# Attention rounds of a two-layer kernel: transposing probabilities on VectorE and moving squares inside SBUF

## The chip, the cores and the metric

The kernel runs on one core of one Trainium2 chip. That core has a matrix engine (TensorE, PE in the profile), three other compute engines (VectorE or DVE, ScalarE or ACT, GpSimd or POOL), and SyncE (SP), which in this program issues all DMA transfers. Each engine takes its instructions in the order in which they were written into its stream and waits at one until its inputs are there. The metric is the device time of the whole program in microseconds: 882.81 us, the median of three runs of the kernel before (882.34 to 883.55).

## The reference

Eight sequences of 128 tokens with 512 features pass two layers, each a cross-attention on a context `ctx_4096` of the same shape and a feed-forward block, every one on a layernormed input and added to the stream:

```python
x = x + _L0_xattn_ref(_layernorm(x, axis=-1), ctx_4096, ...)
x = x + _L0_ffn_ref(_layernorm(x, axis=-1), ...)
x = x + _L1_xattn_ref(_layernorm(x, axis=-1), ctx_4096, mask, ...)
x = x + _L1_ffn_ref(_layernorm(x, axis=-1), ...)
```

What matters here is the second cross-attention. It has 32 query heads of 128 dimensions that share 8 key/value heads (four query heads to a group), with RMS norm on queries and keys, scores plus a mask, softmax, the product with the values, and an output projection from 4096 back to 512. The feed-forward block after it takes 4-bit integer weights with a zero point and a scale for each group of 128 rows: gate, up and down projections of 512 x 1792, and silu(gate) * up between them.

## The kernel before

The first layer and the key/value projections of the second take the first 220 us. Most products are computed to nearly float32 accuracy from float32r halves: a tensor is cut into a high part (a copy in float32r) and a low part (the difference), and `mm3` (L73) makes three matmuls, low x high, high x high and high x low. Such cuts are done by ScalarE and VectorE (`split_fast`) or by POOL alone (`split_pool`).

The second cross-attention runs over 64 units, a unit being one key/value group and one sequence (its 4 query heads at once). `round_(n)` (L749) issues the steps of several units in the order of the list `ROUND` (L738); each entry has an offset, the unit it works for being n plus that offset. The whole stage stands under a manual schedule, so every engine gets its instructions in the order of these calls. The steps of a unit before the change, with the offset at which they run:

- `q_mm` (offset 4): query projection, 12 matmuls of 128 x 512; `q_ssq` (4): squares summed by ScalarE; `q_rms` (3): the inverse root on POOL.
- `q_turn` (3): VectorE scales the queries and transposes them in squares of 32 x 32 (L517, L523) into `qb`. Squares lie transposed, but still on the partitions of their rows.
- `q_write` (3) and `q_read` (2): the squares go to DRAM in one transfer of 256 KB, and come back in four of 64 KB to the partitions where they belong. The read is issued one round after the write.
- `s_mm` (1): four score products (L543), a further round later; `s_max` (1) adds the mask and takes the maximum on VectorE, `s_exp` (1) is ScalarE, `s_norm` (1) divides by the sum, on POOL (L565).
- `p_mm` (1): PE transposes the probabilities, four transposes of 128 x 128 (L570), at the end of the round; `p_cut` (0) cuts them on ScalarE and VectorE (L574, L575) from PSUM.
- `av_mm` (0): three matmuls with the values; `av_cut` (0): the result is cut on ScalarE and VectorE (L591, L592), with a reordering of its columns; `o_mm` (0): the output projection, 12 matmuls; `o_add` (0): the sum into the stream (L604).

The string entries stand for loads and cuts of weights, which are spread over the rounds: `"load"` issues DMAs for the q and o weights and every fourth round for keys and values, `"cut"` cuts weights on POOL, `"int"` and `"sub"` load the integer weights of the feed-forward stage with their zero points and write their difference to DRAM (`int_dma`, `int_sub`). The last four rounds take `TAIL`, which has no `q_mm`. In rounds 53 to 57 and in the last ones the layernorm of finished sequences is woven in, and `fillers` puts the first gate and up units of the feed-forward stage (its first `NE` chunks, for the first four sequences) between the steps. All DMA issues stand in one queue, SP's, in the order of the calls.

The prelude (L791) interleaves the last two groups of keys and values with the first queries. The stage after the attention is the feed-forward block, ordered by `emit` for most chunks and written out by hand for the last ones.

Of the kernel before, what the change touches and what calls it, by code (L numbers as in the profile page):

```python
# [9 lines left out]
F32 = mybir.dt.float32  # L10
# [7 lines left out]
P = 128  # L18
# [21 lines left out]
def tile_layers(ctx: ExitStack, tc: tile.TileContext, t, out: bass.AP):  # L40
# [76 lines left out]
    NE = 3  # L117
# [342 lines left out]
    qps, qss, rqs, qbs, q_d, qTs, sps, nms, sms, prs, tps, pTs, avs, aTs, pos = ({} for _ in range(15))  # L460
# [20 lines left out]
    def k_load(g, hf):  # L481

        kTt[g, hf] = pk.tile([P, NQ, HB, SQ], F32, name="kT")
        for k in range(NQ):
            nc.sync.dma_start(
                kTt[g, hf][k * SQ : (k + 1) * SQ].rearrange("p i b a -> p i (b a)"),
                kT_d[g, hf][:, k, :].rearrange("(i c) e -> c i e", c=SQ),
            )

    def v_load(g, hf):  # L490
        for i, (d, p) in enumerate(((vht, "h"), (vlt, "l"))):
            d[g, hf] = pv.tile([P, HB, HD], F32R, name=f"v{p}")
            nc.sync.dma_start(f32(d[g, hf]).rearrange("p b d -> p (b d)"), v_d[g, hf][i])
# [33 lines left out]
    def q_write(u):  # L527
        q_d[u] = dram.tile([P, NQ, NREP * SQ], F32, name=f"q_d{u}")
        nc.sync.dma_start(q_d[u], qbs.pop(u).rearrange("p j r a -> p j (r a)"))

    def q_read(u):

        qTs[u] = wk.tile([P, NQ, NREP * SQ], F32, name="qT", bufs=8)
        for j in range(NQ):
            nc.sync.dma_start(
                qTs[u][j * SQ : (j + 1) * SQ], q_d[u][:, j, :].rearrange("(i c) e -> c i e", c=SQ)
            )
# [29 lines left out]
    def p_mm(u):  # L567
        tp = tps[u] = ps_tr.tile([P, NQ, P], F32, name="tr")
        for r in range(NQ):
            nc.tensor.transpose(tp[:, r, :], prs[u][:, r, :], ident)  # L570

    def p_cut(u):
        ph, pl = pTs[u] = tuple(pat.tile([P, NQ, P], F32R, name=f"pT_{p}") for p in "hl")
        nc.scalar.copy(ph, tps[u])  # L574
        nc.vector.tensor_tensor(pl, tps[u], f32(ph), ALU.subtract)  # L575
# [10 lines left out]
    def av_cut(u):  # L586
        ah, al = aTs[u] = tuple(pat.tile([P, NREP, P], F32R, name=f"aT_{p}") for p in "hl")

        src = avs[u].rearrange("p i (r a) -> p r i a", a=SQ)
        hp, lp = (x.rearrange("p r (i a) -> p r i a", a=SQ) for x in (ah, al))  # L590
        nc.scalar.copy(hp, src)  # L591
        nc.vector.tensor_tensor(lp, src, f32(hp), ALU.subtract)  # L592
# [18 lines left out]
    def int_dma(m, c):  # L611
        wi, zi = (
            wk.tile([P, NREP, P], F32, name="qT", bufs=8).bitcast(I32).rearrange("p r c -> p (r c)")
            for _ in range(2)
        )
        staged[m, c] = (wi, zi)
        if m == "down":
            nc.sync.dma_start(wi, t["down_w"][c * P : (c + 1) * P, :])
            nc.sync.dma_start(zi, t["down_z"][c : c + 1, :].to_broadcast([P, D]))
        else:  # L620
            cols = slice(c * P, (c + 1) * P)
            nc.sync.dma_start(
                wi.rearrange("p (g c) -> p g c", c=P), t[m + "_w"][:, cols].rearrange("(g p) c -> p g c", p=P)
            )
            nc.sync.dma_start(
                zi.rearrange("p (g c) -> p g c", c=P), t[m + "_z"][:, cols].unsqueeze(0).to_broadcast([P, KT, P])
            )
# [16 lines left out]
    def early_unit(m, g, c):  # L644
# [9 lines left out]
        if g % 2 == 0:  # L654
            et[m, c, g] = wk.tile([P, NREP, P], F32, name="qT", bufs=8).rearrange("p r c -> p (r c)")
            nc.scalar.activation(et[m, c, g], ps, AF.Copy, scale=s)
        else:
            d = et[m, c, g - 1]
            if m == "gate" and g == 1:
                a2 = wk.tile([P, NREP, P], F32, name="qT", bufs=8).rearrange("p r c -> p (r c)")  # L660
                nc.scalar.activation(a2, ps, AF.Copy, scale=s)
                nc.gpsimd.tensor_tensor(d, d, a2, ALU.add)
            else:
                nc.vector.scalar_tensor_tensor(d, ps, s, d, ALU.mult, ALU.add)
# [55 lines left out]
    def norm_turn(b):  # L720
        hf, i = divmod(b, HB)
        if i == 0:
            xn2[hf] = tuple(big.tile([P, KT, TOK], F32R, name=f"xnT_{p}") for p in "hl")
        layernorm_t(xnb[b], *xn2[hf], slice(i * P, (i + 1) * P), ps_q, tag="mm")


    FILL = {(NU - 1, p_cut): 3, (NU - 1, s_norm): 2}
    for n in range(NU - 4, NU - 1):
        FILL[n, p_cut], FILL[n, s_norm] = 1, 3 if n == NU - 2 else 2
    BANKS = "qst" "qst" "qsqt" "qstqs" "tqstqos" "to"  # L730
    xn2, xnb, xst = {}, {}, {}
    norms = {}
    for b in range(NB):
# [5 lines left out]
        (1, s_mm), (3, q_rms), (0, p_cut), (4, q_mm, (0,)), (1, s_max), (0, av_mm), "int", (2, q_read),  # L739
        (0, av_cut), (3, q_turn), (4, q_mm, (1, 2, 3)), (1, s_exp), "load", (3, q_write), "cut", "sub",  # L740
        (0, o_mm), (1, s_norm), (4, q_ssq), (1, p_mm), (0, o_add),
    ]

    TAIL = [
        (1, s_mm), (3, q_rms), (0, p_cut), (1, s_max), (0, av_mm), (2, q_read), (0, av_cut), (3, q_turn),
        (1, s_exp), (1, s_norm), "load", (3, q_write), (0, o_mm), (1, p_mm), (0, o_add),
    ]

    def round_(n):  # L749
        for it in ROUND if n < NU - 4 else TAIL:  # L750
            if isinstance(it, str):
                for fn, a in tasks.get((n, it), []):
                    fn(*a)
            elif 0 <= n + it[0] < NU and not (n == 0 and it[1] is q_read):
                it[1](n + it[0], *it[2:])
# [34 lines left out]
    with tc.manual_schedule():  # L790
        for u, (g, hf) in enumerate(((NG - 2, 0), (NG - 2, 1), (NG - 1, 0))):  # L791
            kv_part(g, hf, 0)
            if u:
                q_rms(u - 1)
                q_turn(u - 1)
                q_write(u - 1)
# [3 lines left out]
            q_ssq(u)  # L800
            if u == 0:
                kv_cut(NG - 1)
            else:
                q_read(u - 1)
                for k in ((0, 1), (2, 3))[u - 1]:
                    load_dma("o", 0, k)
        s_mm(0)
        s_max(0)
        s_exp(0)
        s_norm(0)  # L810
        kv_part(NG - 1, 1, 0)
        q_rms(2)
        q_turn(2)
        q_write(2)
        kv_part(NG - 1, 1, 2)
        q_mm(3, range(KT))
        kv_out(NG - 1, 1)
        q_read(2)
# [9 lines left out]
        for k in range(KT):  # L828
            wo[0, k] = o_first[(k + 1) % KT]
        for k in (0, 1):  # L830
# [4 lines left out]
        p_mm(0)  # L835
# [5 lines left out]
        fillers(len(fill) - 2)  # L841
# [72 lines left out]
    def gated(c):  # L914
        th = ths.pop(c)
        tp = part(th, c)
        nc.vector.tensor_tensor(tp, tp, part(gu["up", 0], c), ALU.mult)
# [3 lines left out]
        nc.scalar.copy(part(hh, c), tp)  # L921
# [37 lines left out]
    def emit(seq, i):  # L959
        c = ORDER[i] if i < NI else NI  # L960
        for it in seq.split():
# [9 lines left out]
            elif k in "SHL" and c < NI:  # L971
                {"S": silu, "H": gated, "L": rest}[k](c)

    for i in range(NI - 1):
# [3 lines left out]
        emit(f"g0 d0 g2 g1 u0 g3 gm d1 u2 {a}u1 d3 d2 u3 um S" + (" H L" if i < NI - 2 else ""), i)  # L978
    ET = mybir.EngineType
    with tc.manual_schedule(engines={ET.PE, ET.DVE, ET.Activation, ET.Pool}):  # L980
# [14 lines left out]
        rest(ORDER[-2])  # L995
        downs("A")
        up_unit("up", 0, c)
        silu(c)
        up_unit("up", 1, c)
# [4 lines left out]
        gated(c)  # L1004
        downs("AV")
# [66 lines left out]
```

## Time and profile before

| | |
|---|---|
| median of three runs | 882.81 us (882.34 to 883.55) |
| the profiled execution: its own time | 884.13 us |
| its span, first to last instruction | 882.3 us |
| PE busy | 852.1 us |
| DVE, POOL, ACT busy | 626.7, 517.5, 438.7 us |
| PE busy from 293 to 629 us (45 rounds) | 335.93 of 336.00 us |
| DMA share in that stretch | 0.74 |
| transposes of probabilities (L570), 256 of them | 40.1 us busy, 279 ns each |
| score products (L543), 512 passes | 68.0 us busy, 276 ns each |

Busy time is the time in which an engine had an instruction in flight. Matmuls overlap on PE, so that the durations of a group add up to more than the group holds PE; what a group costs is read from the distance between the starts of what stands before and after it. A row of a timeline has the start in the span, the duration, engine, line, operation and the tiles written and read; in brackets stands the idle time of the engine before it and what ended it. A DMA row shows the issue on SP (SPq); the time to landing is told from the start of the issue.

### The profile page before, as it was taken

What the parts mean: (1) busy time and instruction counts of PE and PEld (TensorE: products, weight loads), DVE (VectorE), ACT (ScalarE), POOL (GpSimd) and SP (SyncE); (2) the same over time, 40 slices, a digit from 0 to 9 for tenths busy, and PEclk for the clock granted to TensorE, in tenths of its full rate; (3) what the DMA queues carried; (4) which work ended last, traced back from release to release, by engine and by line L of the source; (5) the groups of instructions that cost most, each with busy time, mean ns of one, the idle gap of its engine ahead of it and who ended that gap; (6) DMA issues with size and microseconds to landing.
All of it is one profiled execution on the core that took longest, in us unless ns stands there. A gap on an engine that the chain in (4) does not pass through costs nothing.

```text
span 882.3 us, 14414 instructions
## 1 busy us (share of the span) xinstructions
PE 852.1 (97%) x4568; PEld 716.2 (81%) x4568; DVE 626.7 (71%) x1049; ACT 438.7 (50%) x1565; POOL 517.5 (59%) x571
## 2 busy tenths in 40 slices
PE   6999999999999999999999999999999989999976
PEld 5889999899787888888888888888778767788764
DVE  6613797775766677777777677666786887888877
ACT  5324444243544454455544444445555668666652
POOL 4551684234565455555555555775554568899884
PEclk9999999999999999999999999999999999999999
DMA  8522441435787788878788886644344412222103
GB/s 295 138 96 97 143 145 72 134 105 168 237 253 227 221 245 240 218 242 243 229 237 239 243 238 210 187 145 138 110 129 144 132 34 73 72 72 72 48 13 109
DMA packets 141182, 141.07 MB, mean 160 GB/s; under 512 B 17969, under 2 KB 92465, under 8 KB 141105
## 3 DMA queue, kind: packets, MB, share of 16 engines
q1 hardware_dynamic: 141104, 140.14, 53.3%
q8 instruction: 37, 0.61, 0.3%
q14 instruction: 41, 0.33, 0.1%
HBM read 97.62 MB, written 42.47 MB: 159 GB/s over the span
## 4 chain that ended last, share of the span: by engine, by line
PE 79%; DVE 6%; POOL 5%; DMA 5%; issue 2%; ACT 2%; SPq 1%; DVEq 0%; ACTq 0%; POOLq 0%
PE mm L74 8%; PE mm L76 8%; PE mm L75 8%; PE f L870 6%; PE f L871 6%; PE o L76 6%; PE s L543 6%; PE o L75 6%; PE o L74 6%; PE tr L570 3%; PE kv L76 3%; PE kv L75 3%; PE kv L74 3%; DMA qT<-q_d 2%; PE o L584 1%
## 5 line engine op out<-in xcount | busy, mean ns | idle before, releaser
L565 POOL TENSOR_TENSOR pr<-pr,rs 128x512 f32<-128x512 f32 x64 | 66.6, 1040 | 179.6 <-DVE rs L563 176.7
L604 DVE TENSOR_TENSOR xs<-o,xs 128x512 f32<-128x512 f32 x64 | 44.2, 691 | 95.5 <-PE o L76 95.5
L74 PE MATMUL mm<-wq_l,xnT_h 128*128 128x512 f32 x256 | 105.4, 412 | 0.0
L76 PE MATMUL o<-wo_h,aT_l 128*128 128x512 f32 x256 | 100.0, 391 | 0.7 <-DVE aT_l L592 0.7
L74 PE MATMUL o<-wo_l,aT_h 128*128 128x512 f32 x256 | 100.1, 391 | 0.2 <-DVE wo_l L66 0.2
L76 PE MATMUL mm<-wq_h,xnT_l 128*128 128x512 f32 x256 | 100.2, 391 | 0.0
L75 PE MATMUL mm<-wq_h,xnT_h 128*128 128x512 f32 x256 | 100.0, 391 | 0.0
L75 PE MATMUL o<-wo_h,aT_h 128*128 128x512 f32 x256 | 99.7, 390 | 0.0
L574 ACT CAST pT_h<-tr 128x512 fp32r<-128x512 f32 x64 | 37.5, 585 | 121.2 <-PE tr L570 121.2
L557 ACT ACTIVATE pr<-s,nm 128x128 f32<-128x128 f32 x256 | 90.8, 373 | 3.2 <-DVE nm L551 3.0
L591 ACT CAST aT_h<-o 128x512 fp32r<-128x512 f32 x64 | 37.6, 587 | 106.9 <-PE o L584 106.9
L74 PE MATMUL kv<-wkv_l,cT_h 128*128 128x256 f32 x256 | 73.6, 288 | 0.0
L508 ACT ACTIVATE junkq<-mm 128x128 f32<-128x128 f32 x256 | 67.3, 279 | 12.4 <-PE mm L76 6.1
L76 PE MATMUL kv<-wkv_h,cT_l 128*128 128x256 f32 x256 | 73.3, 286 | 0.0
L75 PE MATMUL kv<-wkv_h,cT_h 128*128 128x256 f32 x256 | 72.9, 285 | 0.0
L543 PE MATMUL s<-kT,qT 128*128 128x128 f32 x512 | 68.0, 276 | 1.9 <-DMA qT<-q_d 1.9
L348 POOL TENSOR_TENSOR rrq<-msq,nhalf 128x4 f32<-128x4 f32 x64 | 64.7, 1011 | 5.3
L543 PEld LDWEIGHTS s<-kT,qT 128*128 128x128 f32 x512 | 62.3, 192 | 3.0 <-DMA qT<-q_d 2.8
L575 DVE TENSOR_TENSOR pT_l<-tr,pT_h 128x512 fp32r<-128x512 f32 x64 | 44.0, 688 | 22.8 <-ACT pT_h L574 22.8
L76 PEld LDWEIGHTS o<-wo_h,aT_l 128*128 128x128 f32 x256 | 48.1, 188 | 11.6 <-DVE aT_l L592 1.5
L76 PEld LDWEIGHTS mm<-wq_h,xnT_l 128*128 128x128 f32 x256 | 48.1, 188 | 10.7
L74 PEld LDWEIGHTS o<-wo_l,aT_h 128*128 128x128 f32 x256 | 48.1, 188 | 10.7 <-DVE wo_l L66 0.6
(234 smaller groups left out, 2445.0 us busy)
## 6 DMA issues: line engine op xcount, KB each, us to landing
q_d<-qb SPq DMA_DIRECT2D x64, 256.0 KB, 2.4
qT<-q_d SPq DMA_DIRECT2D x256, 64.0 KB, 3.1
wst<-in_qpT SPq DMA_DIRECT2D x36, 256.0 KB, 3.5
wst<-in_opT SPq DMA_DIRECT2D x36, 256.0 KB, 3.1
wkv<-in_kvT SPq DMA_DIRECT2D x8, 512.0 KB, 4.3
v_d<-vh SPq DMA_DIRECT2D x16, 256.0 KB, 2.1
v_d<-vl SPq DMA_DIRECT2D x16, 256.0 KB, 2.3
kT_d<-kT SPq DMA_DIRECT2D x16, 256.0 KB, 2.6
```

The source lines that it names most:

```text
L74: nc.tensor.matmul(o, ah, bl, start=start, stop=False)
L75: nc.tensor.matmul(o, ah, bh, start=False, stop=False)
L76: nc.tensor.matmul(o, al, bh, start=False, stop=stop)
L348: nc.gpsimd.tensor_tensor(r[:, :n], ms[:, :n], nhalf[:, :n], ALU.pow)
L508: nc.scalar.activation(junk, qps[u][:, r * HD : (r + 1) * HD], AF.Square, accum_out=ssq[:, r : r + 1])
L543: nc.tensor.matmul(sp[:, r, :], qTs[u][:, r, :], kTt[blocks[j]][:, :, i, :], start=True, stop=True)
L557: nc.scalar.activation(pr[:, r, :], sps[u][:, r, :], AF.Exp, bias=nms[u][:, r : r + 1], accum_out=sm[:, r : r + 1])
L565: nc.gpsimd.tensor_tensor(pr, pr, rs.unsqueeze(2).to_broadcast([P, NQ, P]), ALU.mult)
L575: nc.vector.tensor_tensor(pl, tps[u], f32(ph), ALU.subtract)
L604: nc.vector.tensor_tensor(x, pos[u], x, ALU.add)
L870: nc.tensor.matmul(ps[:, hf, :], w, rl, start=True, stop=False)
L871: nc.tensor.matmul(ps[:, hf, :], w, rh, start=False, stop=True)
```

## The change

- `q_write` and `q_read` become one step `q_move`: four transfers inside SBUF, each from 32 partitions of `qb` to all 128 partitions of one query head's slice of `qT`. It stands at offset 3, in the round of `q_turn`.
- The same way replaces the transposes on PE: `p_turn` lets VectorE transpose the probabilities in squares of 32 x 32, `p_move` makes the four transfers, and `p_cut` takes its input from SBUF, with POOL in place of VectorE for the low part.
- Scores, maximum, exponential and normalization stand at offset 2 in place of 1, so there is a round between normalization and `p_turn`.
- Squares now lie in another order on the partitions; keys and values are loaded in the same order (one transfer for the keys in place of four), and `av_cut` needs no reordering.
- Gate and up integer weights and zero points are laid out by the host so that a chunk is contiguous.
- `NE` is 4 in place of 3: one more chunk of the feed-forward stage has its first half computed early. `FILL` and `BANKS`, which place these fillers, are written anew, the prelude and `TAIL` follow the new offsets, and `cast` is a step of its own in the feed-forward stage.

```diff
-    NE = 3
+    NE = 4
...
     def k_load(g, hf):
-        for k in range(NQ):
-            nc.sync.dma_start(
-                kTt[g, hf][k * SQ : (k + 1) * SQ].rearrange("p i b a -> p i (b a)"),
-                kT_d[g, hf][:, k, :].rearrange("(i c) e -> c i e", c=SQ),
-            )
+        nc.sync.dma_start(
+            kTt[g, hf].rearrange("p i b a -> p i (b a)"), kT_d[g, hf].rearrange("(i c) j e -> (c j) i e", c=SQ)
+        )
...
-    def q_write(u):
-        q_d[u] = dram.tile([P, NQ, NREP * SQ], F32, name=f"q_d{u}")
-        nc.sync.dma_start(q_d[u], qbs.pop(u).rearrange("p j r a -> p j (r a)"))
-
-    def q_read(u):
-        qTs[u] = wk.tile([P, NQ, NREP * SQ], F32, name="qT", bufs=8)
-        for j in range(NQ):
-            nc.sync.dma_start(
-                qTs[u][j * SQ : (j + 1) * SQ], q_d[u][:, j, :].rearrange("(i c) e -> c i e", c=SQ)
-            )
+    def move(dst, src):
+        for i in range(NQ):
+            nc.sync.dma_start(dst[:, i, :], src[i * SQ : (i + 1) * SQ].rearrange("p j i a -> p j (i a)"))
+
+    def q_move(u):
+        qTs[u] = wk.tile([P, NQ, NREP * SQ], F32, name="qT", bufs=6)
+        move(qTs[u], qbs.pop(u))
...
-    def p_mm(u):
-        tp = tps[u] = ps_tr.tile([P, NQ, P], F32, name="tr")
-        for r in range(NQ):
-            nc.tensor.transpose(tp[:, r, :], prs[u][:, r, :], ident)
+    def p_turn(u):
+        pb = pbs[u] = wk.tile([P, NQ, NQ, SQ], F32, name="pb", bufs=1)
+        nc.vector.transpose(
+            pb.rearrange("p j i a -> p i j a"), prs.pop(u).rearrange("p i (j c) -> p i j c", c=SQ)
+        )
+
+    def p_move(u):
+        tps[u] = wk.tile([P, NREP, P], F32, name="pT")
+        move(tps[u], pbs.pop(u))
 
     def p_cut(u):
-        ph, pl = pTs[u] = tuple(pat.tile([P, NQ, P], F32R, name=f"pT_{p}") for p in "hl")
+        ph, pl = pTs[u] = tuple(pat.tile([P, NREP, P], F32R, name=f"pT_{p}") for p in "hl")
         nc.scalar.copy(ph, tps[u])
-        nc.vector.tensor_tensor(pl, tps[u], f32(ph), ALU.subtract)
+        nc.gpsimd.tensor_tensor(pl, tps[u], f32(ph), ALU.subtract)
...
     def av_cut(u):
-        src = avs[u].rearrange("p i (r a) -> p r i a", a=SQ)
-        hp, lp = (x.rearrange("p r (i a) -> p r i a", a=SQ) for x in (ah, al))
-        nc.scalar.copy(hp, src)
-        nc.vector.tensor_tensor(lp, src, f32(hp), ALU.subtract)
+        nc.scalar.copy(ah, avs[u])
+        nc.vector.tensor_tensor(al, avs[u], f32(ah), ALU.subtract)
...
     def int_dma(m, c):
...
+        nc.sync.dma_start(wi, t[m + "_w"][c * P : (c + 1) * P, :])
+        nc.sync.dma_start(zi, t[m + "_z"][c : c + 1, :].to_broadcast([P, D]))
...
-    FILL = {(NU - 1, p_cut): 3, (NU - 1, s_norm): 2}
-    for n in range(NU - 4, NU - 1):
-        FILL[n, p_cut], FILL[n, s_norm] = 1, 3 if n == NU - 2 else 2
+    FILL = {}
+    for n, m in ((NU - 4, 1), (NU - 3, 1), (NU - 2, 2), (NU - 1, 2)):
+        FILL[n, s_max], FILL[n, p_cut] = m, 3
...
     ROUND = [
-        (1, s_mm), (3, q_rms), (0, p_cut), (4, q_mm, (0,)), (1, s_max), (0, av_mm), "int", (2, q_read),
-        (0, av_cut), (3, q_turn), (4, q_mm, (1, 2, 3)), (1, s_exp), "load", (3, q_write), "cut", "sub",
-        (0, o_mm), (1, s_norm), (4, q_ssq), (1, p_mm), (0, o_add),
+        (1, p_turn), (1, p_move), (2, s_mm), (3, q_rms), (4, q_mm, (0, 1)), (2, s_max), (0, av_mm), "int",
+        (0, av_cut), (4, q_mm, (2, 3)), (3, q_turn), (2, s_exp), (3, q_move), "load", "cut", (4, q_ssq),
+        (2, s_norm), "sub", (1, p_cut), (0, o_mm), (0, o_add),
     ]
     TAIL = [
-        (1, s_mm), (3, q_rms), (0, p_cut), (1, s_max), (0, av_mm), (2, q_read), (0, av_cut), (3, q_turn),
-        (1, s_exp), (1, s_norm), "load", (3, q_write), (0, o_mm), (1, p_mm), (0, o_add),
+        (1, p_turn), (1, p_move), (2, s_mm), (3, q_rms), (2, s_max), (0, av_mm), (0, av_cut), (3, q_turn),
+        (2, s_exp), (2, s_norm), (3, q_move), (1, p_cut), "load", (0, o_mm), (0, o_add),
     ]
...
     with tc.manual_schedule():
-        for u, (g, hf) in enumerate(((NG - 2, 0), (NG - 2, 1), (NG - 1, 0))):
+        for u, (g, hf) in enumerate(((NG - 2, 0), (NG - 2, 1), (NG - 1, 0), (NG - 1, 1))):
             kv_part(g, hf, 0)
             if u:
                 q_rms(u - 1)
                 q_turn(u - 1)
-                q_write(u - 1)
+                q_move(u - 1)
+            if u > 1:
+                s_mm(u - 2)
+                s_max(u - 2)
+                s_exp(u - 2)
+                s_norm(u - 2)
...
     def gated(c):
-        th = ths.pop(c)
-        tp = part(th, c)
-        nc.vector.tensor_tensor(tp, tp, part(gu["up", 0], c), ALU.mult)
+        th = hts[c] = ths.pop(c)
+        nc.vector.tensor_tensor(part(th, c), part(th, c), part(gu["up", 0], c), ALU.mult)
+
+    def cast(c):
+        th = hts[c]
         hh, hl = (fh.tile([P, 2, TOK], F32R, name=f"h_{p}") for p in "hl")
```

## The prediction

> **What bounds the kernel now.** First the page: busy times, then the chain that ended last.
>
> ```profile
> PE 852.1 (97%) x4568; PEld 716.2 (81%) x4568; DVE 626.7 (71%) x1049; ACT 438.7 (50%) x1565; POOL 517.5 (59%) x571
> ...
> PE 79%; DVE 6%; POOL 5%; DMA 5%; issue 2%; ACT 2%; SPq 1%; DVEq 0%; ACTq 0%; POOLq 0%
> ```
>
> PE fills the span and carries the chain. A busy PE need not be at its peak, so next one attention round, from the timelines of PE, ScalarE, VectorE and the DMA issues.
>
> ```profile
> 449.72 0.64 PE L570 MATMUL tr<-ident,pr 128*128 128x128 f32 x4
> 450.20 1.06 PE L543 MATMUL s<-kT,qT 128*128 128x128 f32 x8
> 451.01 0.48 PE L74 MATMUL mm<-wq_l,xnT_h 128*128 128x512 f32 x1
> 451.32 0.40 PE L75 MATMUL mm<-wq_h,xnT_h 128*128 128x512 f32 x1
> ...
> 452.25 0.40 PE L584 MATMUL o<-pT_l,vh 128*128 128x512 f32 x1
> ...
> 457.26 0.64 PE L570 MATMUL tr<-ident,pr 128*128 128x128 f32 x4
> 457.73 1.06 PE L543 MATMUL s<-kT,qT 128*128 128x128 f32 x8
> ```
> ```profile
> 452.68 0.59 ACT L591 CAST aT_h<-o 128x512 fp32r<-128x512 f32 x1 [1.70 <-PE o L584]
> ```
> ```profile
> 453.30 0.69 DVE L592 TENSOR_TENSOR aT_l<-o,aT_h 128x512 fp32r<-128x512 f32 x1 [0.26 <-ACT aT_h L591]
> 453.91 0.68 DVE L517 TENSOR_TENSOR q<-mm,rrq 128x512 f32<-128x512 f32 x1
> 454.63 0.71 DVE L523 STREAM_TRANSPOSE qb<-q 128x512 f32<-128x512 f32 x1
> ```
> ```profile
> 449.95 1.79 SPq L535 DMA_DIRECT2D qT<-q_d  x4
> ...
> 455.37 0.34 SPq L529 DMA_DIRECT2D q_d<-qb  x1
> ```
>
> A round is 457.73 - 450.20 = 7.53 us with no PE gap; transposes take 450.20 - 449.72 = 0.48 of it. The other rows show how late in a round the query squares are ready: qb ends at 455.34, 5.1 us after the scores started. They go to DRAM at 455.37, are read from 457.48, and first used by a score product at 465.26: nearly 10 us, a whole round of slack. Last, the views of the two transfers of that detour (the writes' summary, then that of both), and the chain in a stretch where a read did come late.
>
> ```profile
> DMA to landing us min/median/max: 2.0/2.4/5.1
> ```
> ```profile
> DMA to landing us min/median/max: 1.8/3.1/6.6
> ```
> ```profile
> 256.35 3.55 DMA qT<-q_d
> 259.90 0.09 issue
> 259.99 1.14 PE s L543 x8
> ```
>
> No transfer lands under 1.8 us after its issue starts, and PE stands until it does: the score starts 0.09 us after the landing.
>
> **The change, part by part.** *Removed from PE:* four transposes per unit. 64 x 0.48 = 30.7 us, all of it on the bounding engine: the PE part of a round becomes 7.53 - 0.48 = 7.05.
>
> *The query path loses its slack.* In the order of instructions built for the changed kernel, VectorE has aT_l(n), q(n+3), qb(n+3) in a row; SP then issues four moves of 64 KB; and the score products of unit n+3 are the first PE work of round n+1, right behind the 12 output products of round n. So a ring closes within one round: scores, aV of n, aT_h, aT_l, q, qb, four moves, next scores. Before, the read was issued a round later and the score another round later. Each of the four score products waits for one move, and the last decides. Its time, from one start of the fourth product to the next:
> - fourth product to the next matmul: a quarter of the 0.89 us that a score group holds PE (chain), 0.22;
> - two groups of query products come before aV now: first matmul 0.31 (451.32 - 451.01), seven at 0.227, to the start of the last aV product: 1.90;
> - to aT_h 0.43 (452.68 - 452.25), to aT_l 0.62, to q 0.61, to qb 0.72, qb itself 0.71, to SP's issue 0.03: 3.12;
> - SP from the first to the fourth issue: 1.79 less the last one's 0.43, or 1.44 in the next round; 1.40;
> - the landing, L; and 0.09 to the product.
>
> Sum 6.73 + L. L is not shown, since no transfer inside SBUF is in this trace. Nearest rows: a read of 64 KB from DRAM, 1.8 us at best, 3.1 in the median (it stands behind the integer loads of its round); a write of 256 KB to DRAM, 2.0 at best. Without DRAM at either end it may be quicker: I bound L below by 1.3 (half a microsecond off the best row, an estimate) and above by 3.1. I take 1.85, near the quiet 64 KB row, because in the new order the integer loads go out some 3 us before the moves and little is queued ahead. Then a round is 8.58 us, of which PE waits 1.53.
>
> Sum: before, the score products of rounds 0 and 61 start at 220.72 and 686.09 (timeline), 465.4 us for 61 rounds (7.63 with the slower ones, where layernorm transposes join). After: 61 x 8.58 = 523.4, +58.0. The layernorm rounds stay at 8.58: 7.05 plus some 0.6 of transposes is less.
>
> [...]
>
> *VectorE:* loses pT_l (688 ns), gains the turning of the probabilities (qb's 713): nothing. p_turn waits for POOL's pr, and s_max, aT_l and q stand behind it; pr ends about 6.6 after S (the fourth product's start), p_turn runs at 7.5: covered by 0.9.
>
> *POOL:* gains pT_l from SBUF, 1292 ns as for wo_l<-wst. A round is 1.04 + 0.19 + 1.01 + 0.62 + 1.29 + 1.29 = 5.44 of 8.58; the four rounds with two weight cuts 7.35. pT_l ends near S + 7.9, its aV product starts at S + 8.58 + 2.12: 2.8 covered. Free; if the rounds were 7.05, those four would bind.
>
> *SP:* eight moves of 0.475 instead of four reads and a write, 1.6 us more in 8.58; a key load is one issue instead of four (-1.4, every fourth round). The probability moves issue at about S + 8.2, land by 11.5, and ScalarE wants them at S + 14. The integer loads behind them are subtracted a round later. Contiguous integer and key loads shorten the queue, off the path: nothing.
>
> *Ends:* the prelude computes one more score group (+0.9) and no transposes (-0.5). The last rounds save 2 x 0.48. Eight more early gate/up units move two matmuls each (0.45) from the later feed-forward stage into the tail, some into its 2.5 us of PE idle (1.19 and 1.29 near 713): -1 to -2. The reordered casts at the end: -1 to +1, taken as 0. Together -1.6.
>
> Total: +56. The profiled execution took 884.13 (span 882.3), 0.15% above the median 882.81; from the median, 939.
>
> **Clock.** Granted clock is 1.00 from 293 to 629 us with PE full, and 0.94 after 840, where PE works 29.87 of 42.30. [...]
>
> **Rivals.**
> - *The moves come late* (behind loads): L 2.6 to 3.1, rounds of 9.3 to 9.8, 985 to 1015. For: the reads' median of 3.1 under a DMA share of 0.74. Against: the new order issues them apart from the loads.
> - *Quick moves:* L 0.9 to 1.3, 61 x 0.55 to 0.95 below, 880 to 905. No row is that short.
> - *Faster:* the transposes' time is simply saved, PE 7.05 a round, 882 - 31 = 852. It needs 6.73 + L under 7.05, L under 0.32; break-even with 7.63 is L = 0.90. Against: the shortest landing shown is 1.8. For: only that SBUF to SBUF isn't shown.
> - *Probabilities late* (POOL as the bound): 7.35 in four rounds, 1 us in all, and only where the ring doesn't bind.
>
> **How the numbers follow.** Ring with L 1.3 to 2.6: 0.72; late moves 0.17; quick moves 0.06, its lower end about no change; faster 0.04; no change 0.01. Forecast 939. Range 905 (L 1.3) to 990 (L 2.7), leaving out the quick, the faster and half of the late ones. A change under 0.2% can't be told from none here: faster 0.04, same 0.01, slower 0.95.
>
> **What the new profile would show.** PE idle before the score products, released by the DMA qT<-qb, some 1.5 us a round and 90 in all; PE busy near 87%; score groups 8.6 apart; the four moves 1.8 to 2.1 from issue to landing; no L570 transposes; POOL's pT_l without anyone waiting long for it. It is wrong if moves land in under a microsecond, or if another chain (pr to p_turn to q) stretches the ring beyond what I counted.

## The result, and the profile after

The changed kernel takes 1054.48 us (1053.29 to 1057.07, 4 runs) against 882.58 (881.94 to 883.55, 4 runs) of the kernel before: 1.195 times as long, 95% interval 1.192 to 1.198. The forecast was 939, range 905 to 990. The sign was right and the size too small: +172 instead of +56. The profiled execution's span is 1051.5 us, against 882.3.

First the page of the kernel after: busy times, the clock granted to TensorE in 40 slices, the chain of work that ended last (by engine), the score products' group, and the moves (KB each, us from issue to landing).

```profile
PE 927.7 (88%) x4312; PEld 738.1 (70%) x4312; DVE 631.0 (60%) x1054; ACT 429.6 (41%) x1572; POOL 611.2 (58%) x639
...
PEclk9999999998999987998999899989899999999998
...
PE 36%; DMA 16%; DVE 14%; issue 11%; SPq 10%; POOL 8%; ACT 4%; DVEq 0%; POOLq 0%; ACTq 0%
...
L542 PE MATMUL s<-kT,qT 128*128 128x128 f32 x512 | 125.9, 341 | 89.3 <-DMA qT<-qb 74.8
...
qT<-qb SPq DMA_DIRECT2D x256, 64.0 KB, 2.1
pT<-pb SPq DMA_DIRECT2D x256, 64.0 KB, 2.9
```

PE's share of the chain fell from 79% to 36%. What came in is the ring that the prediction names: the moves (DMA), VectorE, SP's issuing. PE stands idle 89.3 us before the score products, 74.8 of them until a move of queries lands. One thing is not of the ring: PE does 256 instructions less, 31 us of work, and yet is busy 75.6 us longer (927.7 against 852.1). The page's groups say where. The score products alone are busy 57.9 us longer (125.9 against 68.0), because they now start one by one: 0.49 us for the two passes of one product (508.70 below), where all eight passes took 1.06 before. The query products are busy 39.5 us longer (345.1 against 305.6, their three groups together). These got slower, and the slices of the clock show when.

Next the timeline of one round of the kernel after, all engines (start, duration; in brackets the idle time before it and what ended that), from one group of score products to the next:

```profile
508.70 0.49 PE L542 MATMUL s<-kT,qT 128*128 128x128 f32 x2 [0.18 <-DMA qT<-qb]
...
510.88 0.40 PE L589 MATMUL o<-pT_l,vh 128*128 128x512 f32 x1
...
511.31 0.59 ACT L593 CAST aT_h<-o 128x512 fp32r<-128x512 f32 x1 [5.89 <-PE o L589]
...
511.93 0.69 DVE L594 TENSOR_TENSOR aT_l<-o,aT_h 128x512 fp32r<-128x512 f32 x1 [1.28 <-ACT aT_h L593]
...
512.54 0.68 DVE L518 TENSOR_TENSOR q<-mm,rrq 128x512 f32<-128x512 f32 x1
...
513.25 0.71 DVE L524 STREAM_TRANSPOSE qb<-q 128x512 f32<-128x512 f32 x1
...
514.03 2.49 SPq L531 DMA_DIRECT2D qT<-qb  x4
...
516.16 0.49 PE L542 MATMUL s<-kT,qT 128*128 128x128 f32 x2 [0.81 <-DMA qT<-qb]
516.83 1.10 PE L542 MATMUL s<-kT,qT 128*128 128x128 f32 x4 [0.17 <-DMA qT<-qb]
518.13 0.79 PE L542 MATMUL s<-kT,qT 128*128 128x128 f32 x2 [0.20 <-DMA qT<-qb]
```

This is the ring, term by term: 2.18 to the last value product, 0.43 and 0.62 to aT_h and aT_l, 0.61 to q, 0.71 to qb, 0.78 to the first issue. The fourth issue starts 1.89 later (514.03 + 2.49 - 0.60 for the last one), and its landing releases the fourth score product 2.21 after that. Sum 9.43 us, from 508.70 to 518.13. Each of the four score products waits for one move: they start as far apart as SP issues the moves, 0.61 to 0.69.

And the clock. The view of windows of the kernel after, on a grid of 3.413 us on which all 32 of its half-clock stretches begin (busy us of PE and matmuls, granted clock, DMA share, GB/s):

```profile
473.72:477.13 3.41, 2.06 (x10) 1.00 0.37 79
477.13:480.55 3.42, 3.32 (x10) 0.50 0.93 262
...
483.96:487.37 3.41, 2.35 (x12) 1.00 0.57 165
...
494.20:497.61 3.41, 2.25 (x10) 1.00 0.43 86
497.61:501.02 3.41, 3.27 (x9) 0.50 0.74 220
...
504.44:507.85 3.41, 2.39 (x11) 1.00 0.29 63
...
514.68:518.09 3.41, 2.14 (x9) 1.00 0.43 102
518.09:521.50 3.41, 3.37 (x9) 0.50 0.96 283
```

In the windows at full clock shown here PE stands 1.02 to 1.35 us idle, in one to four holes, waiting for the moves. Where it was busy 2.06 to 2.25 us of 3.41, the next window ran at half clock; after 2.35 and 2.39 it did not. A round that begins at half clock takes 10.95 us, the next 9.4, then again: 19 such windows between 300 and 700 us, mostly 20.48 apart. From the score products of round 0 (221.46) to those of round 61 (850.27) the kernel now takes 628.8 us; before it was 465.4. That is 163 of the 169 us by which the spans differ.

### The profile page after: what moved, and what is told of

The parts are those of the page before. It is cut to its first block, busy times and chain, and to the rows that moved or that the text cites. A ratio compares the mean times of both kernels' runs of the same rounds, so it can differ in the third digit from the quotient of the medians.

```text
span 1051.5 us, 14424 instructions
## 1 busy us (share of the span) xinstructions
PE 927.7 (88%) x4312; PEld 738.1 (70%) x4312; DVE 631.0 (60%) x1054; ACT 429.6 (41%) x1572; POOL 611.2 (58%) x639
## 4 chain that ended last, share of the span: by engine, by line
PE 36%; DMA 16%; DVE 14%; issue 11%; SPq 10%; POOL 8%; ACT 4%; DVEq 0%; POOLq 0%; ACTq 0%
DMA qT<-qb 12%; SPq L531 10%; PE f L858 5%; PE f L859 5%; PE mm L74 4%; PE mm L75 4%; PE mm L76 4%; PE s L542 4%; DVE q L518 4%; DVE qb L524 4%; ACT aT_h L593 3%; DMA vl<-v_d 2%; DMA pT<-pb 1%; PE o L587 1%; PE o L589 1%
## 5 line engine op out<-in xcount | busy, mean ns | idle before, releaser
L564 POOL TENSOR_TENSOR pr<-pr,rs 128x512 f32<-128x512 f32 x64 | 81.6, 1274 | 249.8 <-DVE rs L562 249.8
L542 PE MATMUL s<-kT,qT 128*128 128x128 f32 x512 | 125.9, 341 | 89.3 <-DMA qT<-qb 74.8
L542 PEld LDWEIGHTS s<-kT,qT 128*128 128x128 f32 x512 | 80.9, 203 | 146.0 <-DMA qT<-qb 132.3
L74 PE MATMUL mm<-wq_l,xnT_h 128*128 128x512 f32 x256 | 119.7, 467 | 0.0
L548 DVE TENSOR_TENSOR s<-s,mask_sb 128x512 f32<-128x512 f32 x64 | 44.6, 697 | 124.4 <-PE s L542 124.4
L75 PE MATMUL mm<-wq_h,xnT_h 128*128 128x512 f32 x256 | 112.8, 441 | 0.0
L76 PE MATMUL mm<-wq_h,xnT_l 128*128 128x512 f32 x256 | 112.6, 440 | 0.0
L594 DVE TENSOR_TENSOR aT_l<-o,aT_h 128x512 fp32r<-128x512 f32 x64 | 44.2, 691 | 111.3 <-ACT aT_h L593 111.1
L580 POOL TENSOR_TENSOR pT_l<-pT,pT_h 128x512 fp32r<-128x512 f32 x64 | 81.0, 1266 | 7.6 <-ACT pT_h L579 7.6
L74 PEld LDWEIGHTS mm<-wq_l,xnT_h 128*128 128x128 f32 x256 | 56.2, 220 | 9.8
```

Source lines behind the costliest of these rows:

```text
L74: nc.tensor.matmul(o, ah, bl, start=start, stop=False)
L75: nc.tensor.matmul(o, ah, bh, start=False, stop=False)
L76: nc.tensor.matmul(o, al, bh, start=False, stop=stop)
L542: nc.tensor.matmul(sp[:, r, :], qTs[u][:, r, :], kTt[blocks[j]][:, :, i, :], start=True, stop=True)
L564: nc.gpsimd.tensor_tensor(pr, pr, rs.unsqueeze(2).to_broadcast([P, NQ, P]), ALU.mult)
L580: nc.gpsimd.tensor_tensor(pl, tps[u], f32(ph), ALU.subtract)
```

## The experiments

In brackets stands the ratio to the kernel before, run beside each version, with its 95% interval.

**Is it the ring through the queries?** Scores that read the queries of the unit before:

```diff
-                sp[:, r, :], qTs[u][:, r, :], kTt[...]
+                sp[:, r, :], qTs[max(u - 1, 0)][:, r, :], kTt[...]
```

> The changed kernel, but each score product reads the queries of the unit before (their moves landed a round earlier); all instructions and transfers stay, the scores are of the wrong unit. Ring theory: the moves of a round no longer release its next scores, PE idle before the score products (now 75 us, released by the moves) nearly vanishes, and rounds fall from 10.3 to the next limit, PE's 7.05 or SP's issues (8 moves at 0.645 plus four others, 7.3 to 7.8): 865 to 925 us. Rival (the probabilities' way over POOL and DMA sets the round): rounds stay at 9.4 or more, over 1000 us.

Measured: 930.78 us (one run), 124 less, and a little above the range expected. Most rounds take 7.03 to 7.06 us (32 of 61 are under 7.2). Up to round 45 every fourth takes 9.5 to 13.5, the one behind the loads of keys and values. Three rounds of PE's timeline, the second of them such a long one, whose value products wait for the split of the probabilities:

```profile
497.45 1.05 PE L542 MATMUL s<-kT,qT 128*128 128x128 f32 x8
504.48 1.05 PE L542 MATMUL s<-kT,qT 128*128 128x128 f32 x8
...
508.86 0.50 PE L587 MATMUL o<-pT_h,vl 128*128 128x512 f32 x1 [1.94 <-ACT pT_h L579]
...
514.65 1.05 PE L542 MATMUL s<-kT,qT 128*128 128x128 f32 x8
...
521.68 1.05 PE L542 MATMUL s<-kT,qT 128*128 128x128 f32 x8
```

The view of waits (us in all, times, the longest):

```profile
ACT pT_h L579 <- DMA pT<-pb: 95.3, 40, 6.5
POOL pT_l L580 <- ACT pT_h L579: 71.5, 36, 5.9
```

So at least 124 of the 172 us come from the query path. Behind it stands a second limit that the prediction had as covered: the moves of the probabilities.

**What is the clock worth?** Seven matmuls that nothing reads fill PE's waits in each round: one before each score product but the first, four after the output products.

```diff
+            if r and 2 < u < NU - 12:
+                idle_mm(1)
...
+        if u < NU - 14:
+            idle_mm(4)
```

> The changed kernel with seven extra matmuls a round that nobody reads, four behind the output projection and one between score products, in PE's waits (1.6 us of work a round, up to round 49). Clock theory: the granted clock, half speed for 3.4 us out of 20.5 in the attention, stays at 1.0; the rounds of 10.9 us become 9.4 to 9.6; 1054 goes down to 995 to 1020, though PE does more. Rival (the dips are where PE waits anyway and cost nothing): unchanged, or longer by up to 50 x 1.6 = 80 us.

Measured: 1036.92 us (1.175, 1.171 to 1.180). More work for PE, and 17.6 us less time. The windows from 300 to 700 us, kernel after and then this one (busy us of PE, PEld, DVE, ACT, POOL, then the clock):

```profile
300.00:700.00 400.00, 343.72 (x1359) 261.62 (x1359) 206.29 (x348) 138.60 (x702) 224.75 (x236) 0.91 0.62 171
```
```profile
300.00:700.00 400.00, 377.42 (x1697) 290.74 (x1696) 214.57 (x362) 146.18 (x738) 236.37 (x247) 1.00 0.63 176
```

The clock is 1.00 throughout, and the term to the last value product falls from 2.92 to 2.14 (means of rounds 10 to 49). But the round only falls from 10.27 to 9.85: the issues of the four moves spread 0.12 more, they land 0.12 later, and the product waits 0.14 longer. Of these 40 rounds 24 take 9.41 in the mean, and 16 still 10.50, at full clock. That a quicker ring meets the other transfers at another point of its round is a guess; it was not tested. The clock went up as expected (1.00 for 0.91), but of the 34 to 59 us expected 17.6 came.

**What are SP's four issues in a row worth?** Two of the four query moves are issued by ScalarE:

```diff
-        move(qTs[u], qbs.pop(u))
+        move(qTs[u], qbs.pop(u), (nc.sync, nc.scalar))
```

> The changed kernel with two of the four query moves issued by ScalarE, so that the last of the four goes out after about 0.65 us and not 1.93. Ring theory: 1.25 us less in each of 61 rounds, some 975 us; down to 930 if the shorter wait also keeps the clock. Rival (DMA engines, not issues, set when the last move lands): within 1% of 1054.

Measured: 990.5 us (1.1225, 1.118 to 1.127), 64 less, where 975 was expected. The spread of the four issues falls from 1.93 to 0.72 a round, the landing rises from 2.17 to 2.84, the ring from 10.27 to 9.18. Issues of this kernel:

```profile
qT<-qb SPq DMA_DIRECT2D x128, 64.0 KB, 2.2
qT<-qb ACTq DMA_DIRECT2D x128, 64.0 KB, 2.6
```

Half of what is won in issuing is lost in landing; why the landing got longer was not followed. The clock dips less often (0.97 from 300 to 700 us), which shows in the term to the last value product: 2.41 for 2.92.

**Are moves inside SBUF dear as such?** The kernel before with its query path alone changed: the four moves in place of the write and the read, scores still one unit ahead, probabilities still transposed by PE. (The keys come in one transfer here too, as the order of the squares demands.)

```diff
-        (2, q_read), ... (3, q_write)
+        (3, q_move)
```

> The kernel before with the query path alone changed: moves inside SBUF in the round of q_turn in place of the detour over DRAM, scores still one unit ahead, probabilities still transposed by PE. The moves then have a round of slack. Ring theory: 875 to 888, as before (883) but for a few us of early waits on the reads. Rival (moves inside SBUF are dear in themselves, by issue time of 0.6 us or contention): 895 or more.

Measured: 881.39 us (879.82 to 882.65, 10 runs), ratio 0.999, 0.9975 to 1.0004: no change. Its chain, and its moves:

```profile
PE 83%; DVE 6%; POOL 5%; ACT 2%; issue 2%; DMA 1%; SPq 0%; DVEq 0%; ACTq 0%; POOLq 0%
```
```profile
qT<-qb SPq DMA_DIRECT2D x256, 64.0 KB, 2.2
```

The same moves, with the same landing, cost nothing where a round of slack lies between them and the score products.

**The slack given back to the changed kernel.** Query products, factor, turning and move one round earlier:

```diff
-        (1, p_turn), (1, p_move), (2, s_mm), (3, q_rms), (4, q_mm, (0, 1)), ... (3, q_turn), ... (3, q_move), ...
+        (1, p_turn), (1, p_move), (2, s_mm), (4, q_rms), (5, q_mm, (0, 1)), ... (4, q_turn), ... (4, q_move), ...
```

> The changed kernel with the query path one round earlier (projection five units ahead, turn and moves four), so that the moves have a round of slack again; the same work, one projection more in the prelude. Ring theory: no PE wait on the query moves; the next limit is SP's queue, 8 moves at 0.645 us, two integer loads, a weight load and a write, 7.3 a round and 9.2 in every fourth (keys, values), 7.8 in the mean against PE's 7.05: 870 to 915 us, PE waiting on late probability moves in the rounds behind key and value loads. If the moves alone were not what held the rounds: 950 or more.

Measured: 932.87 us (1.059, 1.054 to 1.063): 122 us back, with nothing left out, but above the range expected. It looks like the first experiment: 7.03 to 7.06 in many rounds, some near 8, and 9.5 to 13.3 in most of those behind the loads of keys and values:

```profile
ACT pT_h L579 <- DMA pT<-pb: 102.2, 43, 5.3
POOL pT_l L580 <- ACT pT_h L579: 73.0, 37, 4.8
```

**Another order instead of another round.** In the changed kernel, q_turn and q_move go ahead of s_max, so that the query path no longer waits for the value products of its round:

```diff
-        (1, p_turn), (1, p_move), (2, s_mm), (3, q_rms), (4, q_mm, (0, 1)), (2, s_max), (0, av_mm), "int",
-        (0, av_cut), (4, q_mm, (2, 3)), (3, q_turn), (2, s_exp), (3, q_move), "load", "cut", (4, q_ssq),
+        (1, p_turn), (1, p_move), (2, s_mm), (3, q_rms), (3, q_turn), (3, q_move), (4, q_mm, (0, 1)), (2, s_max),
+        (0, av_mm), "int", (0, av_cut), (4, q_mm, (2, 3)), (2, s_exp), "load", "cut", (4, q_ssq),
```

> The changed kernel with one step moved: VectorE turns the queries ahead of the maximum, at the start of the round, and SP issues the moves there; everything stays in its round. The ring then runs over POOL's two-round path (maximum, exponential, normalization, low part, inverse root, turn, moves), 15.2 us for two rounds, 7.6 each, with SP's 7.8 beside it: 880 to 925. If it stays over 1000, the place of the turn in the round was not the cause.

Measured: 990.29 us (one run), a miss. The moves are off the path, and a ring of VectorE and POOL is on it. Its waits from 300 to 700 us:

```profile
POOL pr L564 <- DVE rs L562: 111.8, 46, 2.6
ACT pr L556 <- DVE nm L550: 85.5, 45, 2.2
PEld o L76 <- DVE aT_l L594: 76.0, 45, 2.0
DVE q L518 <- POOL rrq L348: 67.8, 45, 2.6
```

VectorE now stands waiting for POOL's factor with the maxima and aT_l queued behind it, so PE's output products wait for aT_l: about 8.7 us in most rounds.

**The second limit.** The other runs keep the query path a round earlier and try to bring all rounds to 7.05. First, the integer and weight loads from ScalarE's queue at the end of the round:

```diff
-        nc.sync.dma_start(wi, t[m + "_w"][c * P : (c + 1) * P, :])
+        nc.scalar.dma_start(wi, t[m + "_w"][c * P : (c + 1) * P, :])
...
```

> As e5, with the integer and weight loads of the rounds issued by ScalarE at its idle end of the round; SP keeps moves, key and value loads and the write, 6.05 us a round. If SP's queue is the limit of e5, rounds fall to PE's 7.05: 61 x (7.63 - 7.05) = 35 us under the kernel before, 843 to 862, faster than both kernels. If POOL (6 us and gaps), ScalarE's added issues or the DMA engines bind first: 865 or more.

Measured: 932.42 us (1.056, 1.052 to 1.061), no gain over 932.87. The transfers' records say what the second queue left as it was. In the trace of the kernel after, each of the 925 transfers signals its landing on one of eight semaphores, and the program takes the eight in turn, so that all 917 behind the first eight have the one of the transfer eight before. The program of this version deals them out in the same way, to SP's and ScalarE's transfers alike. 900 of those 917 issues carry a wait for that earlier landing. In this trace none of the 917 goes out sooner, 28 go out within 0.2 us of it, and never more than eight transfers are under way; in the 905.70 us version below it is again none that goes out sooner, and 103 within 0.2 us. So a load ahead of a move can hold the move's semaphore until it lands. This limit is the program's. What the chip would take beyond eight no run shows, and a version with more semaphores was not tried.

The keys, high and low parts of the values in three rounds instead of one:

```diff
...
-        at(max(HB * j - 5, 1), "load", v_load, g, hf)
+        at(max(HB * j - 4, 1), "load", v_load, g, hf, (0,))
+        at(max(HB * j - 3, 1), "load", v_load, g, hf, (1,))
```

> The query path a round earlier as in the kernel with four rounds of lead, and the five or so transfers of a key and value block spread over three rounds: keys in the first, value high parts in the next, value low parts in the one after. Theory A (every fourth round of 9.5 to 13 us is made by the three big loads of one round, 0.75 MB together, which stand in front of the probabilities' moves): the excess of about 4.5 us in 15 rounds shrinks to a third or less, so 870 to 890 us. Theory B (the rounds are long because a transfer may only be issued once the one eight before it has landed, so that any load in front of the moves delays them, wherever it is put): the excess is spread over three rounds instead of one and the sum stays, 915 to 935 us.

Measured: 922.86 us (1.045, 1.042 to 1.048). Theory B: most long rounds of 9.5 to 13 went, and the others rose to about 8. Then the order as well: write-backs a round later, the big loads between the probabilities' moves and the queries', and the two integer loads issued by ScalarE:

```diff
+        (1, p_turn), (1, p_move), "out", "load", (2, s_mm), (4, q_rms), (5, q_mm, (0, 1)), (2, s_max), (0, av_mm),
+        (0, av_cut), (5, q_mm, (2, 3)), (4, q_turn), (2, s_exp), (4, q_move), "cut", (5, q_ssq),
+        (2, s_norm), "sub", (1, p_cut), "int", (0, o_mm), (0, o_add),
...
```

> As the run before, with the order of the transfers changed too: the write-back of the integer weights is issued a round after its subtraction, right behind the probabilities' moves, the weight, key and value loads follow it, so that the four query moves end the round, and the two integer loads are issued by ScalarE late in the round. Theory A (moves are late only because of what is issued in front of them in the same stretch): all rounds come to PE's own 7.05 us, 61 rounds take 430 us against 465 before, and the time is 845 to 865 us. Theory B (eight transfers before each one must have landed, whichever queue): 8 moves and 4 to 7 other transfers a round leave a move about half a round to land, rounds of 7.1 to 9 us, 880 to 925 us. Theory C (POOL, with its product at 1.3 us in place of 1.04, is next to PE): about 7.5 us a round, 870 to 885 us.

Measured: 905.70 us (1.025, 1.0195 to 1.030; its four times spread from 899.03 to 908.06), within theory B's range and the best version of the changed kernel that leaves nothing out. Many rounds are 7.03 to 7.06 now, those beside loads 7.5 to 11. SP's issues in one of the latter:

```profile
402.85 0.45 SPq L471 DMA_DIRECT2D wst<-in_qpT  x1
403.34 0.52 SPq L493 DMA_DIRECT2D vl<-v_d  x1
403.97 2.52 SPq L532 DMA_DIRECT2D qT<-qb  x4
407.12 4.37 SPq L532 DMA_DIRECT2D pT<-pb  x4
```

The first move of probabilities goes out at 407.12, the second at 409.37. The weight load issued at 402.85 landed at 407.05 and the value load of 403.34 at 409.35: they held the semaphores of the first and the second move.

Four attempts at the rest failed. The split of the moved probabilities at the start of the round that uses it:

```diff
-        (1, p_turn), (1, p_move), "out", ... "sub", (1, p_cut), "int", ...
+        (1, p_turn), (1, p_move), (0, p_cut), "out", ... "sub", "int", ...
```

> As the kernel with the new order of transfers, and one step moved: the split of the moved probabilities (its two instructions on ScalarE and POOL) opens the round whose value products use it, in place of ending the round before, so that the four moves of probabilities have about 3 us more to land. Theory A (the 61 rounds from the first one of the loop took 475.6 us there, 45 over PE's 7.05 each, because the moves land up to 5 us after their issue while loads are in flight, and a little slack absorbs that): the rounds fall to 435 to 450 us and the time to 865 to 882 us. Theory B (the transfers as a whole are too many for the round: each is issued only when the one eight before has landed, and slack only moves the wait): within 8 us of the run before, 898 to 912 us.

Measured: 915.91 us (1.039, 1.036 to 1.042), slower than both theories. The integer units spread over 56 rounds, on top:

```diff
-        at(i + 1, "int", int_dma, m, c)
+        at(1 + i * 4 // 3, "int", int_dma, m, c)
...
```

> As the run before, with the integer weights' 42 units (two loads and a write-back each, 768 KB in all) spread over 56 rounds in place of 42. Theory A (slack settles it): within 5 us of the run before. Theory B (the number of transfers in a round settles it): one unit less in every fourth round takes three of 12 to 15 transfers out of it; the long rounds get shorter in a quarter of the cases, 5 to 15 us less than the run before.

Measured: 923.32 us (1.046, 1.043 to 1.049), slower again, against both theories: more rounds at 7.05, and a few of 12 to 15. Why it is slower was not followed up. Two buffers for the squares of the probabilities (on top of the late split):

```diff
-    ppr = pool(l1s, "ppr", 2)
+    ppr = pool(l1s, "ppr", 1)
...
-        pb = pbs[u] = wk.tile([P, NQ, NQ, SQ], F32, name="pb", bufs=1)
+        pb = pbs[u] = wk.tile([P, NQ, NQ, SQ], F32, name="pb", bufs=2)
```

> As the kernel in which the split of the moved probabilities opens the round, with two buffers for the probabilities' squares in place of one (the exponentials' tile gives up its second for it). Theory A (there the transposition of the next squares by VectorE waits until the four moves have read the only buffer, so a late move holds VectorE, and with it the maxima and the queries, and the slack given to the moves is taken back): rounds of 10 to 13 us beside loads go to 8 to 9, and the time to 875 to 895 us. Theory B (ScalarE is held instead, since its two integer loads can only be issued when the transfer eight before has landed and the write-back of an older tile too): the time stays within 8 us of 916.

Measured: 916.07 us (1.037, 1.032 to 1.043): nothing. The exponentials gave up their second buffer for it, so the run shows that the trade brings nothing, not what a second buffer alone would do. And the integer loads back on SP, at the end of the round:

```diff
-        nc.scalar.dma_start(wi, t[m + "_w"][c * P : (c + 1) * P, :])
+        nc.sync.dma_start(wi, t[m + "_w"][c * P : (c + 1) * P, :])
...
```

> As the run before, with the two integer loads issued by SP at the end of the round, behind the query moves, in place of ScalarE. Theory A: SP's queue gets longer again, so the moves of the next round are issued later; within 8 us of the run before or up to 10 us slower. Theory B (ScalarE's own waits to issue are what is left): 15 to 35 us less than the run before, 865 to 890 us, and below the kernel before if it falls under 881.

Measured: 924.57 us (1.047, 1.045 to 1.049), 8.5 more: taking the loads off ScalarE brought nothing, with SP's queue longer by them.

Last, bytes against number, both from the 905.70 version. Fewer bytes in as many transfers, and as many bytes in one transfer more:

```diff
-        nc.scalar.dma_start(zi, t[m + "_z"][c : c + 1, :].to_broadcast([P, D]))
+        nc.scalar.dma_start(zi[:, 0:P], t[m + "_z"][c : c + 1, 0:P].to_broadcast([P, P]))
...
```

> The kernel with the new order of transfers (905.7 us), but of each unit's zero points only the first 128 of 512 columns are loaded, and used for all four groups of columns (so the integer weights and all that follows from them are another result): the number of transfers is the same, and 192 KB of about 1.5 MB a round are gone from the rounds that load integer weights. Theory A (the bytes of a round set its length beside loads: the attention moves about 200 GB/s here as in the kernel before, which is near what the mix allows): 192 KB at 200 GB/s are 0.96 us in 42 rounds, so up to 35 us less, 870 to 890 us. Theory B (the number of transfers sets it, since each is issued only when the one eight before has landed): landings hardly change, 895 to 910 us.

```diff
-        nc.scalar.dma_start(zi, t[m + "_z"][c : c + 1, :].to_broadcast([P, D]))
+        for h in (slice(0, D // 2), slice(D // 2, D)):
+            nc.scalar.dma_start(zi[:, h], t[m + "_z"][c : c + 1, h].to_broadcast([P, D // 2]))
```

> The kernel with the new order of transfers, with the zero points of each unit loaded by two transfers of 128 KB in place of one of 256 KB: the same bytes, one transfer more in 42 rounds. Theory A (bytes): within 6 us of 905.7. Theory B (number of transfers): one of 13 more in a round, some 0.5 us in 42 rounds, 918 to 930 us.

Measured: 892.91 us (1.012, 1.010 to 1.014) with fewer bytes, 920.50 (1.045, 1.041 to 1.049) with one transfer more: 12.8 less and 14.8 more, 0.30 and 0.35 us in each of the 42 rounds. Theory B has the second right; the first lies between the two. The 200 GB/s of theory A was no ceiling: windows shown above reach 262 and 283. Waits for the probabilities' moves from 250 to 700 us in the 905.70 version, with fewer bytes, and with one transfer more:

```profile
ACT pT_h L580 <- DMA pT<-pb: 76.0, 41, 5.7
```
```profile
ACT pT_h L580 <- DMA pT<-pb: 57.0, 35, 5.2
```
```profile
ACT pT_h L580 <- DMA pT<-pb: 100.5, 45, 4.6
```

Both move the same wait. This fits eight transfers under way at most: one transfer more takes one of the eight places, and more bytes may hold one longer. The second half of this is the author's reading, which no run shows by itself. No version of the changed kernel beat the kernel before.

Not all that is left lies in the rounds. In the 905.70 version's trace the 61 rounds take 475.6 us against 465.4; the span is 19.3 longer, and of that 3.3 lie ahead of round 0 and 5.8 behind round 61. With fewer bytes the rounds take 463.0, less than before the change, and the version is still slower, by 3.8 ahead of them and 6.8 behind.

## Why the prediction was right in sign and wrong in size

*Removed from PE*: right. With the ring opened, the rounds that wait for nothing else take 7.03 to 7.06; the step had 7.05.

*The query path loses its slack*: right as a mechanism. With the ring opened 122 to 124 of the 172 us go, and with slack the moves are free (0.999). Its sum, 8.58, was mis-sized. Means over 61 rounds, in us, from the trace of the kernel after; the predicted values are in brackets:

| Term | Measured | Predicted | Excess |
|---|---|---|---|
| fourth score product to last value product | 2.83 | (2.12) | 0.71 |
| to aT_l | 1.06 | (1.05) | 0.01 |
| q and qb, to qb's end | 2.08 | (2.04) | 0.04 |
| to the first issue | 0.07 | (0.03) | 0.04 |
| SP, first to fourth issue | 1.92 | (1.40) | 0.52 |
| landing of the fourth | 2.18 | (1.85) | 0.33 |
| to the product | 0.15 | (0.09) | 0.06 |
| round | 10.30 | (8.58) | 1.72 |

61 x 1.72 = 105 us; with the 58 foreseen, the 163 measured. Three terms failed.

- *SP from the first to the fourth issue.* The price was taken from reads out of DRAM, 1.79 for four. Four moves inside SBUF take 2.49: 0.60 each, not 0.43.
- *The landing, L.* 2.18 against 1.85 taken. The reason given for 1.85 was that little is queued ahead of the moves. That held: the median is 2.1, and none of the 256 lands under 2.07, so the excess is not a queue's. The row it was taken from, a read out of DRAM, was of another kind of transfer.
- *Clock*, in the first term. The sum allows nothing for it. But the clock halved after windows of 3.41 us in which PE was busy 2.06 to 2.25. Spread evenly over time, the 0.94 that the prediction read after 840 us would have been 0.13 a round on its 2.12 us up to the last value product (an estimate). In the windows shown the half clock falls on the stretch right behind the wait, the query products, which lie on the ring. In rounds 10 to 49 that term is 2.92, and 2.14 with the waits filled: 0.78 a round, six times as much. (Of these 40 rounds 20 have 3.67 there in the mean and 20 have 2.18.)

A fourth, smaller miss: rounds 0 and 1 take 12.06 and 14.84 us, some 6 more than two others, in places that *Ends* did not look at. In round 0 POOL splits two output weights (3.9 us) before the factor of the next queries. Round 1 ends with a wait for keys. The scores moved a round ahead, but the second block's keys are still issued in round 1, at 244.40; they land at 248.68, and unit 4's scores start at 248.82, 4.0 us after the last of their moves landed (244.79). Outside the 61 rounds *Ends* had -1.6 (with the small end of its own -1 to -2), and the trace has +6: 0.7 ahead of round 0 (221.46 against 220.72), and the rest behind round 61. From there to the first product of the feed-forward stage the kernel now takes 36.1 us, before 29.9; the stage itself is 1.3 shorter. What holds the last rounds was not followed.

*VectorE* and *POOL*: free while the ring binds, as said. POOL's pr was costed at 1040 ns as before; it takes 1274 in the mean (1379 from 300 to 700 us). The step counted four rounds with two weight cuts; rounds 2 and 3 have two as well. Neither cost anything while the ring bound.

*SP*: the moves of the probabilities were costed at nothing, covered because they land 2.5 us before ScalarE wants them. That held in the changed kernel, where ScalarE waits for them 13.4 us in all. Without the cover of a long round they are the next limit, 95 to 102 us of waiting. The step said when they land, and not what they cost once the ring is gone.

*Rivals*: the time lies nearest to "the moves come late", but for another reason. Except in a few rounds they did not come late behind loads; SP issued them slower and PE lost clock. "Faster" needed L under 0.32.

*What the new profile would show*: idle before the score products 89.3 us (said: 90) and PE at 88% (87) agreed by accident: the round was longer, and PE slower at its work. Groups 8.6 apart were 9.4 and 10.95.

## What to carry to other kernels

A transfer put between two engines costs its issue, its landing and its place among the transfers under way: here 0.60 us, 2.1 us and one of eight. The query moves were free with a round of slack behind them (0.999), so when scores or loads move ahead, move what feeds them ahead by as much. Price each new transfer by one of its own kind, issue and landing apart, or by the upper bound. Look at which semaphores a transfer waits for before it is issued: a second queue that shares them brought nothing (932.42 us against 932.87). Where a bounding engine will start to wait in every round, ask what its clock does in the windows with the holes: here waits of 1.02 to 1.35 us in a window went with a half clock behind some of them, 0.78 us more a round.

## What was not expected of the hardware

- Half clock behind short waits: 3.41 us at 0.50 after windows in which PE was busy 60 to 66%. No one figure of busy time parts the cases: in the version with the early turn, windows with 2.02, 2.03 and 2.13 us busy were followed by clock 1.00; in the one with the split issue, 1.51 and 1.90 by 0.50. What it goes by stays open.
- More work took less time: seven idle matmuls a round, 17.6 us less.
- A move of 64 KB inside SBUF took SP 0.60 us to issue and landed 2.1 us after the start of its issue; the same size read from DRAM took 0.43 to issue. The price is not the transfer's alone: the load of an output weight from DRAM takes 0.43 right behind such a read and 0.59 right behind a move (medians).
- Score products of the same shape were longer, 341 ns in the mean instead of 276; that goes with the half clock and the single starts.
- POOL's product of the probabilities was longer beside one step of VectorE. The 42 of 64 that overlap VectorE's subtraction of the zero points (L624) take 1.40 us, the 22 others 1.04. In the kernel before none overlapped, and all took 1.04.
